# Bringing the last tiles' outputs to their tokens: scatter and reload, or products with one-hot matrices

## The chip, the cores and the metric

The kernel runs on one core of a Trainium2 chip. A core has a matrix engine (TensorE, "PE"; its weight loads are "PEld"), a vector engine (VectorE, "DVE"), an engine for activation functions (ScalarE, "ACT"), a general engine (GpSimd, "POOL") and a queue engine (SyncE, "SP"), each with its own program, kept together by semaphores. Sixteen DMA engines move data between HBM, where inputs and outputs lie, and SBUF, the on-chip memory of 128 partitions. PE writes to PSUM, a second on-chip memory of eight banks; DVE and ACT read it.

The metric is the time of one execution on the device in microseconds (us). A profiled execution lists every instruction with its start and duration, in us from the span's start.

## The reference, cut to what matters

There are 8 batches of 256 tokens with 128 channels, all float32. Two blocks follow one another. The first adds attention-pooled tokens that went through eight experts with a threshold on the gates; in the second each token is adapted, normalised (`xn`; the adapted token is also the `residual`) and sent to its two best of eight experts:

```python
x = x + _L0_ffn_ref(_L0_cond_ref(x, ...), ...)
x = x + _L1_ffn_ref(_L1_cond_ref(x, itok_B_0_8, ...), ...)
...
    probs = jax.nn.softmax(jnp.einsum('bld,de->ble', xn, gate_w), axis=-1)
    w, idx = jax.lax.top_k(probs, TOP_K)
    w = w / jnp.sum(w, axis=-1, keepdims=True)
    cw = jnp.sum(w[..., None] * jax.nn.one_hot(idx, E, dtype=x.dtype), axis=2)
    h = jax.nn.gelu(jnp.einsum('bld,edh->eblh', xn, w1) + b1[:, None, None, :], approximate=False)
    out_e = jnp.einsum('eblh,ehd->ebld', h, w2) + b2[:, None, None, :]
    output = jnp.einsum('ble,ebld->bld', cw, out_e)
    return output + residual
```

So each of the 2048 output tokens is a residual plus two expert outputs, each multiplied by its weight.

## The kernel before, in words

The first block runs densely: 16 tiles of 128 tokens in five units (`UNITS`), every expert for every token, with two stages of products a unit (`layer`, lines 872 to 907). As units end, `adapt` (line 649) normalises their tokens, picks the two experts of each, and GpSimd scatters each token twice into a buffer `xs` in HBM, sorted by expert. With each copy go the row of the output buffer `ys` where its result belongs (`xt[:, D]`) and its weight (`xt[:, D + 1]`). Row number 2 * token + s of `ys` holds the s-th of a token's two results, so the even number next to it names the token.

The second block is sparse. Tiles of 128 sorted rows of one expert are listed as they fill: `SLOTS` is the number of tiles known after units 2, 3 and 4 (17, 21, 39). At most 39 tiles can be needed; the program runs the first 36 (`SURE`) always, and the last three inside a branch (`tc.If`, line 1074) on the count of tiles. A tile goes through four functions:

- `fetch` (line 920): SP loads the tile's rows from `xs` (64 KB and a little) and the expert's first weights (256 KB).
- `turn` (line 955): PE transposes, DVE scales into `xc` and copies the bias `b1`.
- `hidden` (line 964): DVE makes `b2`, PE four products `hps`, ACT four Gelu `hs`.
- `output` (line 977): PE four products `yps`, DVE adds bias and weight into `yt` (line 985), and GpSimd scatters the 128 rows of `yt` into `ys` (line 986).

A product of 128x128 by 128 columns in float32 stands in the trace as two PE instructions. In the main loop a tile is fetched five tiles ahead (`LEAD`) and its stages run two tiles apart (`AHEAD`); a planner orders the engines' work by its own costs there. When the loop over 36 tiles ends, `hidden` of tiles 34 and 35 and `output` of 32 to 35 are left.

The full tiles of the early batches come first in the lists. From tile 31 on (`SETTLED`) none of the outputs belongs to the first six batches (`EARLY`). So, once tile 30's scatter has landed, SP loads these six batches' rows of `ys` (`load`, line 1002, 256 KB a batch), and DVE adds both results to the residual (`add`, line 1009, two additions of 128x256). After the scatter of tile 35 come: three stores on SP, the branch over the spare tiles, the loads of the last two batches in halves on SP and ACT, the other three stores, the additions of the four halves, and their stores.

From line 1057 on an order written out by hand (`tc.manual_schedule`) holds for DVE, ACT and POOL; PE and SP stay with the planner. Every engine's queue runs in order: an SP instruction that waits holds back all stores and loads behind it.

Of the kernel before, what the change touches and what calls it, by code (L numbers as in the profile page):

```python
# [22 lines left out]
B, S, D = 8, 256, 128  # L23
P = 128
NT = B * S // P
NG = 4
GT = NT // NG
GN = GT * P
# [16 lines left out]
NSLOT = SLOTS[NU - 1]  # L45
SURE = 36
EARLY = 6


SETTLED = max(SLOTS[NU - 2] + E, 4 * EARLY + E - 1)  # L50
NOWHERE = 1 << 20
SEARCH = 16
SEARCH_GAP = 3
# [30 lines left out]
def tile_adaln_ffn_d2(ctx: ExitStack, tc: tile.TileContext, x, ptype, lang, cols, b1v,  # L84
                      w10, w20, w11d, w21d, lw1, lw2, lgb, out):
    nc = tc.nc
# [25 lines left out]
    ident = const.tile([P, P], F32, name="ident")  # L112
# [478 lines left out]
    for e in range(E):  # L591
        nc.sync.dma_start(out=w21[:, e, :], in_=w21d[e].rearrange("p c d -> p (c d)"))
    nc.sync.dma_start(out=b2all.rearrange("p e d -> p (e d)"),
                      in_=b2d.rearrange("e d -> (e d)").partition_broadcast(P))
    rows = xs.rearrange("(p m t) c -> p m (t c)", p=P, t=GT)
    nc.sync.dma_start(out=rows, in_=empty.rearrange("p t c -> p (t c)").unsqueeze(1).to_broadcast(list(rows.shape)))

# [357 lines left out]
    def turn(k, xt, wt):  # L955
        tp = pss.tile([P, P], F32, tag="sm", name=f"xtp{k}")
        nc.tensor.transpose(tp, xt[:, :D], ident)  # L957
        xc = work.tile([P, P], F32, tag="xc", name=f"xc{k}", bufs=AHEAD + 3)
        nc.vector.tensor_scalar(xc, tp, col[:, C_LG:C_LG + 1], col[:, C_LB:C_LB + 1], ALU.mult, ALU.add)  # L959
        b1 = small.tile([P, HC], F32, tag="b1", name=f"b1_{k}", bufs=AHEAD + 3)  # L960
        nc.vector.tensor_copy(b1, b1all[:, bass.ds(number(k), 1), :].rearrange("p o c -> p (o c)"))  # L961
        return k, xt, wt, xc, b1

    def hidden(k, xt, wt, xc, b1):
        hp = psb.tile([P, HC, P], F32, tag="big", name=f"hps{k}")
        hT = work.tile([P, HC, P], F32, tag="scr", name=f"hs{k}", bufs=NSCR)

        b2 = work.tile([P, GN], F32, tag="gbc", name=f"b2_{k}", bufs=4)[:, :D]
        nc.vector.tensor_tensor(b2, b2all[:, bass.ds(number(k), 1), :].rearrange("p o d -> p (o d)"),
                                xt[:, D + 1:D + 2].to_broadcast([P, D]), ALU.mult)  # L970
        for c in range(HC):
            nc.tensor.matmul(hp[:, c, :], lhsT=wt[:, c * P:(c + 1) * P], rhs=xc, start=True, stop=True)  # L972
        for c in range(HC):
            nc.scalar.activation(hT[:, c, :], hp[:, c, :], AF.Gelu, bias=b1[:, c:c + 1])  # L974
        return k, xt, hT, b2

    def output(k, xt, hT, b2):
        ek = expert(k, PE)
        yp = psy.tile([P, D], F32, tag="y", name=f"yps{k}")
        for c in range(HC):  # L980
            nc.tensor.matmul(yp, lhsT=hT[:, c, :], rhs=w21[:, bass.ds(ek, 1), c * D:(c + 1) * D],  # L981
                             start=(c == 0), stop=(c == HC - 1))

        yt = first.tile([P, HC, D], F32, tag="w2", name=f"yt{k}")[:, 0, :]
        nc.vector.scalar_tensor_tensor(yt, yp, xt[:, D + 1:D + 2], b2, ALU.mult, ALU.add)  # L985
        move = nc.gpsimd.indirect_dma_start(  # L986
            out=ys, out_offset=bass.IndirectOffsetOnAxis(ap=xt.bitcast(I32)[:, D:D + 1], axis=0),
            in_=yt, in_offset=None, bounds_check=2 * NT * P - 1, oob_is_err=False)
        tc.declare_no_dep(move.ins, group="outputs", reason="no two outputs share a row")
        tc.add_to_no_dep_group("outputs", move.ins)  # L990
        if k >= SETTLED:
            tc.declare_no_dep(move.ins, group="settled", reason="no more outputs for the first batches")
        if k == SETTLED - 1:
            for n in range(EARLY):
                load(n, slice(0, 2), nc.sync, "settled")
# [6 lines left out]
    def load(n, part, queue, group=None):  # L1002
        y = work.tile([P, 2, 2 * D], F32, tag="scr", name=f"yg{n}_{part.start}", bufs=NSCR)[:, part, :]
        move = queue.dma_start(out=y, in_=yv[n, :, part, :])
        if group:
            tc.add_to_no_dep_group(group, move.ins)
        loaded.append((n, part, y))

    def add():
        n, part, y = loaded.popleft()  # L1010
        o = resid[n // 2][:, n % 2 * 2 + part.start:n % 2 * 2 + part.stop, :]

        tc.keep_in_program_order(nc.vector.tensor_tensor(o, y[:, :, :D], o, ALU.add))
        tc.keep_in_program_order(nc.vector.tensor_tensor(o, o, y[:, :, D:], ALU.add))
        return n, part, o

    def store(queue, n, part, o):
        tc.keep_in_program_order(queue.dma_start(out=of[n][:, part, :], in_=o))

    fetched, flipped, hid = deque(), deque(), deque()  # L1020

    def proceed(ahead, between=lambda: None):
        if len(flipped) > ahead:
            hid.append(hidden(*flipped.popleft()))
        between()
        if len(hid) > ahead:
            output(*hid.popleft())
# [20 lines left out]
    for k in range(PRIMED, SURE):  # L1048
        ahead(k + LEAD)
        if k == SLOTS[NU - 2]:  # L1050

            while len(flipped) > 1 or len(hid) > 1:
                proceed(1)
        flipped.append(turn(*fetched.popleft()))
        pump()
        proceed(AHEAD, pump)

    ending = ExitStack()
    ending.enter_context(tc.manual_schedule(engines={DVE, ACT, POOL}))
    while flipped or hid:  # L1060
        if flipped:
            hid.append(hidden(*flipped.popleft()))
        while len(hid) > bool(flipped) + 1:
            output(*hid.popleft())
        if not flipped:
            output(*hid.popleft())
    while behind:
        pump()
    sums = [add() for _ in range(EARLY)]
    for _ in range(3):  # L1070
        store(nc.sync, *sums.pop(0))
    more = nc.values_load(tiles[0][0:1, 0:1], engines=(SP, PE, DVE, ACT, POOL), min_val=0, max_val=NSLOT,
                          skip_runtime_bounds_check_because="a count of tiles")
    with tc.If(more > SURE - SLOTS[NU - 2]):
        for k in range(SURE, NSLOT):
            output(*hidden(*turn(*fetch(k))))
    ending.close()
    queues = itertools.cycle((nc.sync, nc.scalar))
    for n in range(EARLY, B):
        for t in range(2):  # L1080
            load(n, slice(t, t + 1), next(queues))
    queues = itertools.cycle((nc.scalar, nc.sync))
    for done_sum in sums:
        store(next(queues), *done_sum)
    while loaded:
        store(next(queues), *add())


# [48 lines left out]
```

## Time and profile before

| what | value |
| --- | --- |
| median of 6 runs | 361.79 us (360.47 to 363.86) |
| profiled execution, its own time | 364.55 us |
| span of its instructions | 362.5 us |
| mean granted PE clock | 0.975 |
| busy PE / DVE / ACT / POOL | 337.5 / 202.7 / 155.9 / 97.0 us |
| moved by DMA | 47.19 MB, 130 GB/s on average |

The profile page divides the span into 40 slices and shows each engine's busy share of a slice in tenths, with the granted PE clock in tenths of full speed. A timeline lists instructions as start, duration, engine, source line, operation, output and inputs, how many were merged, and the idle time of the engine before with what ended it. The chain of waits goes back from the last instruction to what released each step. A window's row has the stretch, its length, the busy time of PE, PEld, DVE, ACT and POOL (with the number of instructions), the granted clock, the share of time the DMA engines were busy, and GB/s. Starts and ends of PE instructions are modelled: its records overlap, and their spacing tells more than their length.

### The profile page before, as it was taken

The numbers are of one execution on the slowest core, as the hardware profiler recorded it, in microseconds if no ns is written. First come the engines' busy times: TensorE is split into PE (matmuls) and PEld (weight loads), VectorE is DVE, ScalarE is ACT, GpSimd is POOL, SyncE is SP. The second block draws the span as 40 slices with busy tenths as digits, with TensorE's granted clock in tenths as the row PEclk, the third lists the DMA queues.
The fourth block names the chain that finished last, engine by engine and source line by source line (L and its number), as shares of the span: only waits on it lengthen the run. The fifth ranks groups of instructions, "written<-read, shape, count | busy, mean of one in ns | idle before, by whom it ended". The sixth has DMA issues, their size and how long they took to land.

```text
span 362.5 us, 5961 instructions
## 1 busy us (share of the span) xinstructions
PE 337.5 (93%) x1628; PEld 222.6 (61%) x1628; DVE 202.7 (56%) x868; ACT 155.9 (43%) x354; POOL 97.0 (27%) x150
## 2 busy tenths in 40 slices
PE   8999999999999999999999999998999877999930
PEld 7885444444444444444445688876879777999920
DVE  3674755623046666575512474786787656544453
ACT  4375455445434343324433355435544514564610
POOL 7500000000000120650170021073136563545540
PEclk9999999999999999999999999999999996999985
DMA  6882799907023210221120111124653654676174
GB/s 191 278 284 74 216 375 380 322 7 201 31 87 104 63 38 29 66 53 56 32 66 22 29 31 44 31 74 114 192 158 94 175 154 109 199 198 199 56 238 136
DMA packets 35417, 47.19 MB, mean 130 GB/s; under 512 B 5562, under 2 KB 18446, under 8 KB 35384
## 3 DMA queue, kind: packets, MB, share of 16 engines
q1 hardware_dynamic: 31640, 41.26, 37.9%
q0 software_dynamic: 2304, 4.37, 3.5%
q10 hardware_dynamic: 1440, 1.18, 1.0%
q8 instruction: 14, 0.23, 0.3%
q14 instruction: 19, 0.16, 0.2%
HBM read 32.66 MB, written 14.39 MB: 130 GB/s over the span
## 4 chain that ended last, share of the span: by engine, by line
PE 79%; DVE 8%; POOL 3%; issue 3%; DMA 2%; another core or an unknown queue 2%; ACT 1%; DVEq 0%; POOLq 0%; SPq 0%
PE hp_first L897 28%; PE yp_first L877 26%; PE yps L981 7%; PE hps L972 7%; PE poolp L358 2%; POOL xs L784 2%; PE idle L219 1%; ACT hs L974 1%; DMA ys<-yt,xt 1%; PE g0p L254 1%; DMA yg<-ys 1%; PE xtp L957 1%; PE xTp L231 1%; DVE sofar L756 1%
## 5 line engine op out<-in xcount | busy, mean ns | idle before, releaser
L899 ACT ACTIVATE hT_first<-hp_first,col 128x512 f32<-128x512 f32 (+1 forms) x160 | 92.6, 602 | 93.8 <-PE hp_first L897 90.0
L897 PE MATMUL hp_first<-poolT,w 128*128 128x512 f32 (+1 forms) x320 | 119.9, 512 | 0.8 <-ACT hT_first L899 0.8
L877 PE MATMUL yp_first<-hT_first,w 128*128 128x512 f32 (+1 forms) x320 | 119.7, 512 | 0.0
L897 PEld LDWEIGHTS hp_first<-poolT,w 128*128 128x128 f32 x320 | 58.6, 190 | 45.7 <-issue 40.4
L877 PEld LDWEIGHTS yp_first<-hT_first,w 128*128 128x128 f32 x320 | 58.7, 190 | 45.3 <-issue 41.0
L974 ACT ACTIVATE hs<-hps,b 128x128 f32<-128x128 f32 x144 | 40.0, 376 | 40.9 <-PE hps L972 10.9
L784 POOL DMA_INDIRECT xs<-zr,pos x32 | 31.6, 986 | 66.0 <-DVE pos L782 30.9
L986 POOL DMA_INDIRECT ys<-yt,xt x36 | 36.6, 1018 | 38.0 <-DVE yt L985 26.3
L981 PE MATMUL yps<-w,hs 128*128 x288 | 39.6, 284 | 2.7 <-DVE ek L627 1.5
L972 PE MATMUL hps<-xc,wt 128*128 128x128 f32 x288 | 39.8, 281 | 2.4 <-issue 2.4
L865 DVE SCALAR_TENSOR_TENSOR part_first<-yp_first,col,gbc_first 128x512 f32<-128x512 f32 (+1 forms) x28 | 17.2, 614 | 40.7 <-PE yp_first L877 39.4
L981 PEld LDWEIGHTS yps<-w,hs 128*128 128x128 f32 x288 | 36.5, 199 | 3.3 <-ACT hs L974 3.0
L972 PEld LDWEIGHTS hps<-xc,wt 128*128 128x128 f32 x288 | 36.0, 196 | 3.2 <-issue 3.1
L550 POOL TENSOR_TENSOR rstd_l<-ve_l,nhalf 128x4 f32<-128x4 f32 (+1 forms) x5 | 5.0, 1008 | 69.0 <-DVE ve_l L548 68.0
L867 DVE TENSOR_TENSOR acc_first<-acc_first,part_first 128x512 f32<-128x512 f32 (+1 forms) x35 | 20.1, 580 | 0.5
L961 DVE COPY b<-col 128x4 f32 x36 | 6.5, 185 | 23.2 <-ACT hs L974 20.1
L985 DVE SCALAR_TENSOR_TENSOR yt<-yps,xt,b 128x128 f32<-128x128 f32 x36 | 12.4, 348 | 10.9 <-PE yps L981 10.3
L484 POOL DMA_DIRECT2D gd_L<-gT_L x1 | 0.7, 668 | 63.9 <-DVE gT_L L482 63.9
L885 ACT ACTIVATE y_first<-yp_first,col 128x512 f32<-128x512 f32 x8 | 5.5, 687 | 23.2 <-PE yp_first L877 14.6
L959 DVE TENSOR_SCALAR xc<-xtp,col 128x128 f32<-128x128 f32 x36 | 14.4, 402 | 0.8 <-PE xtp L957 0.4
L499 DVE TENSOR_SCALAR_CACHE_REDUCE fl<-logit,tr 128x128 bf16<-128x128 f32 x46 | 13.5, 343 | 0.6
L518 DVE TENSOR_SCALAR_CACHE_REDUCE ok<-kt 128x3 f32<-128x3 f32 (+1 forms) x16 | 2.6, 160 | 13.8 <-PE kt L502 13.8
(224 smaller groups left out, 296.7 us busy)
## 6 DMA issues: line engine op xcount, KB each, us to landing
wt<-in_w_dram SPq DMA_DIRECT2D x36, 256.0 KB
xs<-empty SPq DMA_DIRECT2D x1, 8580.0 KB
w<-in_w_dram SPq DMA_DIRECT2D x24, 256.0 KB
gbc_first<-gd_L SPq DMA_DIRECT2D x24, 256.0 KB
xt<-xs SPq DMA_DIRECT2D x36, 65.0 KB
gbc_first<-gd_L SPq DMA_DIRECT2D x16, 128.0 KB
yg<-ys SPq DMA_DIRECT2D x6, 256.0 KB
xg<-in_x_dram SPq DMA_DIRECT2D x8, 128.0 KB
```

Source lines behind the costliest of these rows:

```text
L499: nc.vector.tensor_scalar(flags, lflat, values[:, i:i + 1], None, ALU.is_lt, ALU.add, accum_out=c[:, i:i + 1])
L784: move = nc.gpsimd.indirect_dma_start(out=xs, out_offset=bass.IndirectOffsetOnAxis(ap=pos[:, t:t + 1], axis=0), in_=zr[s][:, t, :], in_off ...
L865: nc.vector.scalar_tensor_tensor(part, y, bias, gbc, ALU.add, ALU.mult)
L867: nc.vector.tensor_tensor(accs[u], accs[u], part, ALU.add)
L877: nc.tensor.matmul(yp, lhsT=w2s[e][:, c, :], rhs=hT[:, c, :], start=(c == 0), stop=(c == HC - 1))
L897: nc.tensor.matmul(hp, lhsT=w1s[e][:, c * P:(c + 1) * P], rhs=sources[g][:, o * P:o * P + n], start=True, stop=True)
L899: nc.scalar.activation(hT[:, c, :], hp, act, bias=col[:, cb1 + e * HC + c:cb1 + e * HC + c + 1])
L959: nc.vector.tensor_scalar(xc, tp, col[:, C_LG:C_LG + 1], col[:, C_LB:C_LB + 1], ALU.mult, ALU.add)
L972: nc.tensor.matmul(hp[:, c, :], lhsT=wt[:, c * P:(c + 1) * P], rhs=xc, start=True, stop=True)
L974: nc.scalar.activation(hT[:, c, :], hp[:, c, :], AF.Gelu, bias=b1[:, c:c + 1])
L981: nc.tensor.matmul(yp, lhsT=hT[:, c, :], rhs=w21[:, bass.ds(ek, 1), c * D:(c + 1) * D], start=(c == 0), stop=(c == HC - 1))
L986: move = nc.gpsimd.indirect_dma_start(out=ys, out_offset=bass.IndirectOffsetOnAxis(ap=xt.bitcast(I32)[:, D:D + 1], axis=0), in_=yt, in_off ...
```

## The change

The last three tiles that always run (33 to 35, from `PLACED = SURE - 3` on) no longer scatter. Instead:

- `turn` of such a tile calls `home`: DVE makes, from the row numbers, a one-hot matrix of 128 rows by the 512 tokens of the last two batches (the even row number is compared with a table `places`, written once by an iota on POOL before tile 30's `turn`).
- `brought` multiplies, on PE, the transposed one-hot slices with `yt`: four products a tile, which add up in two PSUM banks (`late`), one a batch.
- The rows of `ys` of the last two batches are filled with zeros at the start, since not all of them will be written; SP loads them, whole batches at a time, after tile 32's scatter.
- `gathered` joins on PE: identity times residual, identity times the first results, identity times the second, 128x256 each, into PSUM. Of the six early batches the first four are still added on DVE, the other two (`ADDED = 4`) are joined in this way in banks of their own; of the last two, the joins go on in the banks of `brought`. ACT copies three of the four results out of PSUM, DVE the last.
- The tile count is read inside the main loop, the branch over the spare tiles comes last, after all these stores; inside it the spare tiles' outputs go through `brought` too, are added and stored again.
- The hand-written order now holds for PE and SP as well.

In the diff, the conditions on `k >= PLACED` stand in `turn`, after `xc`, and in `output`, after `yt`.

```diff
+PLACED = SURE - 3
+LATE = B - EARLY
+ADDED = 4
...
+    for n in range(EARLY, B):
+        nc.sync.dma_start(out=ys[n * 4 * P:(n + 1) * 4 * P, :].rearrange("(p t) d -> p t d", t=GT), in_=empty[:, :, :D])
...
+        if k >= PLACED:
+            home(k, xt)
...
+        if k >= PLACED:
+            return k, yt
...
+    def gathered(sums, begin):
+        n, part, y, o = taken_up()
+        for i, some in enumerate((o, y[:, :, :D], y[:, :, D:])):
+            nc.tensor.matmul(sums, lhsT=ident, rhs=some, start=begin and not i, stop=i == 2)
+        return n, o
...
+    def home(k, xt):
+        even = small.tile([P, 1], I32, tag="even", name=f"even{k}", bufs=2)
+        nc.vector.tensor_scalar(even, xt.bitcast(I32)[:, D:D + 1], -2, None, ALU.bitwise_and)
+        at = small.tile([P, 1], F32, tag="atf", name=f"atf{k}", bufs=2)
+        nc.vector.tensor_copy(at, even)
+        homes[k] = work.tile([P, GN], F32, tag="acc", name=f"home{k}", bufs=3)
+        nc.vector.tensor_scalar(homes[k], places[0], at, None, ALU.is_equal)
+    def brought(k, yt, sums, begin, end=False):
+        for i in range(GT):
+            nc.tensor.matmul(sums[i // 2][:, i % 2, :], lhsT=homes[k][:, i * P:(i + 1) * P], rhs=yt,
+                             start=begin and i % 2 == 0, stop=end and i % 2 == 1)
...
-    while flipped or hid:
...
-    sums = [add() for _ in range(EARLY)]
-    for _ in range(3):
-        store(nc.sync, *sums.pop(0))
+    hid.append(hidden(*flipped.popleft()))
+    output(*hid.popleft())
+    placed = [output(*hid.popleft())]
+    hid.append(hidden(*flipped.popleft()))
+    store(nc.sync, *add())
+    for n in range(EARLY, B):
+        load(n, slice(0, 2), nc.sync)
+    placed.append(output(*hid.popleft()))
+    late = pairs("late")
+    brought(*placed[0], late, True)
+    store(nc.sync, *add())
+    placed.append(output(*hid.popleft()))
+    brought(*placed[1], late, False)
+    brought(*placed[2], late, False)
+    for _ in range(ADDED - 2):
+        store(nc.sync, *add())
+    for _ in range(ADDED, EARLY):
+        held = psy.tile([P, 2, D], F32, tag="y", name=f"held{loaded[0][0]}")
+        n, o = gathered(held, True)
+        nc.scalar.copy(o, held)
+        store(nc.sync, n, o)
+    lasts = [gathered(some, False) for some in late]
+    for (n, o), some, copy, queue in zip(lasts, late, (nc.scalar.copy, nc.vector.tensor_copy), (nc.scalar, nc.sync)):
+        copy(o, some)
+        store(queue, n, o)
     with tc.If(more > SURE - SLOTS[NU - 2]):
+        rest = pairs("rest")
         for k in range(SURE, NSLOT):
-            output(*hidden(*turn(*fetch(k))))
+            brought(*output(*hidden(*turn(*fetch(k)))), rest, k == SURE, k == NSLOT - 1)
+        for (n, o), some in zip(lasts, rest):
+            nc.vector.tensor_tensor(o, some, o, ALU.add)
+            store(nc.sync, n, o)
     ending.close()
-    queues = itertools.cycle((nc.sync, nc.scalar))
-    for n in range(EARLY, B):
-        for t in range(2):
-            load(n, slice(t, t + 1), next(queues))
-    queues = itertools.cycle((nc.scalar, nc.sync))
-    for done_sum in sums:
-        store(next(queues), *done_sum)
-    while loaded:
-        store(next(queues), *add())
```

More of the change, by code (lines that the diff above doesn't have):

```diff
@@ L50 @@
 SETTLED = max(SLOTS[NU - 2] + E, 4 * EARLY + E - 1)
+PLACED = SURE - 3
+LATE = B - EARLY
+ADDED = 4
+assert PLACED >= SETTLED and LATE * 2 == GT
 NOWHERE = 1 << 20
@@ L1009, in add, with taken_up, store, pairs @@
     def add():
-        n, part, y = loaded.popleft()
[L1011 to L1018, printed above, removed]
+        n, part, y, o = taken_up()
+        nc.vector.tensor_tensor(o, y[:, :, :D], o, ALU.add)
+        nc.vector.tensor_tensor(o, o, y[:, :, D:], ALU.add)
+        return n, o
+    def taken_up():
+        n, part, y = loaded.popleft()
+        return n, part, y, resid[n // 2][:, n % 2 * 2:n % 2 * 2 + 2, :]
+    def gathered(sums, begin):
+        n, part, y, o = taken_up()
+        for i, some in enumerate((o, y[:, :, :D], y[:, :, D:])):
+            nc.tensor.matmul(sums, lhsT=ident, rhs=some, start=begin and not i, stop=i == 2)
+        return n, o
+    def store(queue, n, o):
+        queue.dma_start(out=of[n], in_=o)
+    homes = {}
+    def home(k, xt):
[9 more added lines that the diff above has]
+                             start=begin and i % 2 == 0, stop=end and i % 2 == 1)
+    def pairs(name):
+        return [psb.tile([P, 2, D], F32, tag="big", name=f"{name}{i}") for i in range(LATE)]
+    places = []
     fetched, flipped, hid = deque(), deque(), deque()
@@ L1053, in tile_adaln_ffn_d2 @@
                 proceed(1)
+        if k == SETTLED - 1:
+            places.append(work.tile([P, GN], F32, tag="part", name="places"))
+            tc.keep_in_program_order(nc.gpsimd.iota(
+                places[0], pattern=[[4 * P, LATE], [2, 2], [4, P]], base=EARLY * 4 * P, channel_multiplier=0,
+                allow_small_or_imprecise_dtypes=True))
+            more = nc.values_load(tiles[0][0:1, 0:1], engines=(SP, PE, DVE, ACT, POOL), min_val=0, max_val=NSLOT,
+                                  skip_runtime_bounds_check_because="a count of tiles")
         flipped.append(turn(*fetched.popleft()))
@@ L1056, in tile_adaln_ffn_d2 @@
         proceed(AHEAD, pump)
-    ending = ExitStack()
-    ending.enter_context(tc.manual_schedule(engines={DVE, ACT, POOL}))
-    while flipped or hid:
[L1061 to L1066, printed above, removed]
     while behind:
         pump()
-    sums = [add() for _ in range(EARLY)]
-    for _ in range(3):
-        store(nc.sync, *sums.pop(0))
@@ L1072, in tile_adaln_ffn_d2 @@
-    more = nc.values_load(tiles[0][0:1, 0:1], engines=(SP, PE, DVE, ACT, POOL), min_val=0, max_val=NSLOT,
-                          skip_runtime_bounds_check_because="a count of tiles")
+    ending = ExitStack()
+    ending.enter_context(tc.manual_schedule(engines={PE, DVE, ACT, POOL, SP}))
+    hid.append(hidden(*flipped.popleft()))
[5 more added lines that the diff above has]
+        load(n, slice(0, 2), nc.sync)
```

## The prediction

> **What bounds the kernel now.** I read the busy slices first, then the chain of waits over the last 18 us, then the timelines of DVE, POOL and SP there, and last the windows of that stretch. The slices say that TensorE (PE) is full until the 38th of 40 and then stops, so everything up to about 344 us is PE's and the rest is a tail:
>
> ```profile
> PE   8999999999999999999999999998999877999930
> PEclk9999999999999999999999999999999996999985
> ```
>
> The tail's chain, from the last matmuls on:
>
> ```profile
> 344.54 2.20 PE yps L981 x16
> ...
> 346.99 0.35 DVE yt L985
> ...
> 349.90 4.31 DMA ys<-yt,xt
> ...
> 354.80 3.60 DMA yg<-ys
> ...
> 359.28 0.29 DVE resid L1014
> ```
>
> The reader sees two DMA flights, 4.3 and 3.6 us, one after the other: tile 35's scatter lands at 354.21, only then are the last two batches' rows loaded, and 359.57 + 2.9 of store and closing make the span of 362.5. From the last matmul (ends 348.35) to the end it is 14.2 us without PE. The timeline shows who else uses the DMA engines then:
>
> ```profile
> 342.17 1.08 POOL L986 DMA_INDIRECT ys<-yt,xt  x1 [1.47 <-DVE yt L985]
> 344.53 2.74 SPq L1004 DMA_DIRECT2D yg<-ys  x6
> 344.90 0.97 POOL L986 DMA_INDIRECT ys<-yt,xt  x1 [0.37 <-issue]
> 351.38 0.42 DVE L1013 TENSOR_TENSOR resid<-yg,resid 128x256 f32<-128x256 f32 x1 [1.03 <-issue]
> 356.95 0.29 DVE L1013 TENSOR_TENSOR resid<-yg,resid 128x128 f32<-128x128 f32 x1 [2.31 <-DMA yg<-ys]
> ```
>
> Tile 30's scatter starts at 342.17 and lets the six early loads go at 344.53. Tile 32's starts at 344.90, under these loads. DVE idles 1.03 us before the third early batch: it came at 351.4. The windows give the DMA engines' load (last two columns):
>
> ```profile
> 348.50:352.00 3.50, 0.00 (x0) 0.00 (x0) 2.37 (x7) 0.00 (x0) 1.95 (x2) 0.93 0.87 308
> 352.00:354.30 2.30, 0.00 (x0) 0.00 (x0) 2.20 (x7) 0.00 (x0) 0.00 (x0) 0.50 0.23 77
> ```
>
> They are nearly full until 352, with the six early loads.
>
> **The change part by part.** All times are of the profiled execution: span 362.5, its own time 364.55, that is 0.8% over the median of 361.79. I work out a difference in it and take that from the median.
>
> *Main loop.* Two zero fills (256 KB each) go ahead of the fill of xs on SP. At the 360 GB/s of 55 to 72 us they cost 1.5 us, at a third of it 4.4; the queue is empty (5 GB/s) from 72 to 74 and the next work on it, the gate rows, starts at 80.8. Hidden, and 4.4 us still fit. The iota (128x512) on POOL is put between scatters: nearest rows 0.64 us (affine_select of 128x512) and 0.18 (iota of 39 columns); POOL spends 1.27 of each 1.89 us a tile, so 0.64 is made up within two tiles. The load of the tile count moves to tile 30: 0.27 to 0.51 us an engine (its rows at L1072), hidden on ACT, POOL, SP and DVE, and PE reads one such number per tile already. It leaves SP's wait of the tail, where it cost 1.3 us with its branch but ran out just as the scatter landed. `home` gives DVE three more instructions in each of tiles 33 to 35: 0.15 (128x1, L520), 0.16 (128x1, L522) and 0.69 (128x512, L863), 1.0 us a tile. DVE sat idle 2.43 us before 341.55 and 1.60 before 344.27 waiting for PE, so two fit there; the third delays yt of tile 32, by 0 to 1.0 us. I take 0.3. Without that cover it would be 1.0 more on scatter 32.
>
> *Scatters 33 to 35 go.* Three POOL instructions of 0.97 + 0.30 and the 4.31 us flight leave the chain. What the late loads wait for is now tile 32's scatter. Its landing is bounded by the fastest row, 342.17 to 344.5 (2.4 us, DMA engines idle), and the slowest, 349.90 to 354.21 (4.3 us, under loads). It flies under the six loads, so I take 4.3: 344.90 + 0.3 + 4.3 = 349.5, from 347.3 to 350.2. SP also stands behind the first add (0.85 us after early load 1 lands; 349.5 at the latest, by DVE's own row). So the late loads issue at 349.6 and 350.0 instead of 354.35: 4.7 us earlier.
>
> *But they queue.* Six early batches of 256 KB are ahead on the same queue. Third landed at 351.4; at 308 GB/s a batch is 0.85 us, so by rate the fifth lands at 353.1, the sixth at 353.9, late ones at 354.8 and 355.6. The 77 GB/s after 352 says most of the bytes were through by then, which puts the fifth as early as 352. Lower end for the late ones: 349.6 + the 4.05 us that 354.35 to 358.40 shows, 353.65. I take 352.6 for the fifth and 354.5 for the late ones. That they go out on SP alone and not on SP and ACT: two issues of 0.36 after one another instead of beside, inside the wait for data.
>
> The Trainium skill, page "DMA: Bandwidth & Descriptors", section "Issuing engines are not separate DMA queues", says the same of the queues: DMAs of whichever engine share the 16 DMA engines, so the change of queue should neither win nor lose bandwidth. Our row does not separate the two queues; by the page this edit is 0.
>
> *PE's new work.* After tile 34's output, PE puts four products (128x128 fp32) for each placed tile: as many as hps, x8 in 0.89 us, so 2.7 us for three. They wait for yt33 (346.72 to 347.05 in the trace, where PE had run dry at 346.3), yt34 behind add 0 on DVE (348.3), and yt35 behind add 1 (349.5 + 0.85 + 0.35 = 350.7), so the third ends at 351.6. Before the fifth load (352.6), PE thus waits: all this is hidden. Then two early and two late batches, three products of 128x256 each, six instructions. By the 128x512 and 128x256 rows of the first layer (88.8 us for 192; 31.1 for 128) and the spacing of 0.111 for 128 columns, a 256-column instruction is 0.22 to 0.24 us: 1.38 us a batch. The residual product of batch 5 runs ahead, so from 352.6: 0.92 + 3 x 1.38 = 357.7. The late loads (354.5 + 0.92 + 1.38 = 356.8) are not the limit; PE's order is. This replaces two DVE adds of 0.3 us a half batch, which ended 0.9 us after the last load: the join on PE is the dearer one, and PE begins the late batches only after the early two.
>
> *Behind it.* PE to DVE under 0.1 us when PE has run dry (yps ends at 348.35, yt starts at 348.39), copy of 128x256 from PSUM 0.42 (DVE rows of that shape): 358.2, against 359.57. ACT's copies of batches 5 to 7 (0.41 each, its 128x256 copy) run beside. Then 2.95 us to the end as now, plus two things: the last store is 128 KB instead of 64 KB (64 KB more at the last slice's 136 GB/s are 0.5 us, with the queue empty nearer 0; I take 0.3), and the branch over the spare tiles now comes after the stores. On SP the branch and its seven semaphore steps spread over 353.03 to 354.04, 1.0 us; part runs beside the store's flight, part may come behind its landing: 0 to 1.0, taken 0.4.
>
> Sum: 358.2 + 2.95 + 0.3 + 0.4 = 361.85 against 362.5: 0.65 us won, of 4.7 us by which the loads start earlier. 361.79 - 0.65 = 361.1.
>
> A rule against the change: the skill's page "TensorE: Matmul & The Clock Gate", section "Part 1: The HAM clock gate", says that PE's clock is halved after an idle window of about 3.4 us. The trace agrees: PE is busy 1.2 of the 4 us from 298 to 302, and the granted clock is 0.65 in 300 to 301 and 0.50 after it; in the old tail it is 0.93 in 348.5 to 352 and then 0.50. By the rule a wait of 1 us before the joins costs nothing, and one beyond 3.4 us doubles them.
>
> **The rivals.**
>
> *Loads do not hold the joins (faster).* Without three scatters and two stores among them the early loads may land back to back, the fifth before 351. Then PE goes through from the third placed tile: yt35 at 350.0, its products until 350.9, 4 x 1.38 = 356.4, copy at 357.1, end at 357.1 + 2.95 + 0.3 = 360.4 with the branch beside the store; with add 1 a further 1 us earlier, 359.4. That is 2.1 to 3.1 won: 358.7 to 359.7. For it: 77 GB/s after 352, a thin remainder. Against it: the idle 1.03 us on DVE at 351.4, at a time when the DMA engines show 0.87 busy.
>
> *PE goes cold (slower).* If PE idles long before the joins, the eight-instruction group that takes 1.06 us takes 2.05, as at 301.88 (clock 0.50). The 5.06 us of joins after 352.6 would become 9.7: +4.7, 365.8 by the median. It decides once PE has waited some 3 us, that is with the fifth load at 354.6 or later. Against it: between 346 and 351.6 PE has 3.6 us of work, more than the 1.2 of 4 that went with the drop.
>
> *Signals of PE come late (slower).* In the trace ACT starts hs of tile 35 at 346.55, 2.0 us after its products ended (344.5), and DVE waits 1.9 and 2.4 us in the same way; each time PE was streaming on. If the joins run in one stream the held batches' copies all fall behind it: three ACT copies (1.2 us) and three stores on SP in order (0.36 each) instead of one. Then the last store leaves about 1.1 us later and the gain of 0.65 turns into 0.45 lost: 362.2, and with the longest such wait of DVE, 2.4 us, on top: 364.6.
>
> *Nothing is moved.* The late loads are behind the early ones anyway, and join and branch eat the rest: 361.8, inside the main case.
>
> **How the numbers follow.** Main case (with the last rival in it) 0.46; its own range is 359.6 to 362.6, from the fifth load at 352.0 or 353.1 (-0.6, +0.5), 0.22 or 0.24 us an instruction (-0.2, +0.2), and the ends of store (-0.3, +0.2) and branch (-0.4, +0.6). Loads not holding the joins 0.31. Cold PE 0.08, late signals 0.15. Half a per cent, about what a measurement of this kernel can tell, is 1.8 us: 359.98 and 363.6. Faster: the second case, 0.31. Slower: cold PE and two thirds of late signals, 0.18. Same: the main case and the rest of late signals, 0.51. The range runs from the far end of the second case to the middle of late signals' span and leaves out cold PE: 358.6 to 364.0.
>
> **What would show it.** Right: late loads issued near 350; no scatter after tile 32; PE waiting for yg near 352, its last join ending near 357.5 at a clock of 1.00; the last PSUM copy on DVE near 358. Wrong: yg in SBUF before PE finishes the placed tiles (faster), a granted clock of 0.50 in 352 to 358, ACT's copies bunched behind the last join, a scatter 32 that lands after 351, or tile 31's products on PE later than 340.8, which would mean that the main loop was disturbed.

## The result, and the profile after

The changed kernel takes 364.6 us (median of 24 runs, 361.64 to 369.13), against 361.65 for the kernel before (50 runs on the same chip, 359.90 to 363.86). The ratio is 1.0079, with a 95% interval of 1.0063 to 1.0096: 2.95 us slower, where 0.65 us faster was forecast, and 0.6 us beyond the upper end of the range. By the prediction's own bound of half a per cent this is "slower". That had a chance of 0.18, but on the strength of two reasons in the tail, not of the one that came true. The ratio leaves out the run of 369.13 us, which lies 2% above the fastest.

The two profiled executions alone would have said the opposite: the changed kernel's span is 360.6 us and its own time 362.35, the other's were 362.5 and 364.55. The difference lies in a stretch that the change does not touch. In the windows view (stretch, length, busy PE, PEld, DVE, ACT, POOL with counts, granted clock, DMA share, GB/s) the kernel before shows

```profile
290.00:310.00 20.00, 15.71 (x111) 15.06 (x111) 11.63 (x61) 6.62 (x24) 9.94 (x11) 0.83 0.51 140
```

and the changed one

```profile
290.00:310.00 20.00, 15.98 (x123) 15.33 (x123) 11.71 (x60) 7.17 (x27) 10.73 (x11) 0.91 0.46 134
```

PE stands idle in parts of this stretch, and the clock drops, in one execution further than in the other. Counted by `yt`, which each tile makes once, the kernel before is 0.3 us behind at the tenth tile (293.34 against 293.00) and 2.6 behind at the 25th (330.09 against 327.54). From there to the end the changed kernel takes 33.1 us and the other 32.4, so this pair shows only 0.65 us of the loss. So whole profiles say little here; stretches do.

The changed kernel's busy slices, to be compared with those in the prediction:

```profile
PE   7999999999999999999999999998999976999895
...
PEclk9999999999999999999999999999999998999999
```

The old tail of nearly empty PE slices is gone, as foreseen. New is the 8 in slice 38 of 40 (333.6 to 342.6 us): inside the main loop, where the kernel before had nines from slice 35 to 38. By windows, before:

```profile
330.00:340.00 10.00, 9.90 (x89) 9.74 (x88) 5.67 (x23) 5.35 (x20) 5.35 (x6) 1.00 0.50 153
```

and after:

```profile
330.00:340.00 10.00, 8.18 (x70) 7.67 (x69) 5.72 (x25) 4.38 (x16) 4.62 (x5) 1.00 0.45 129
```

PE stands still for 1.82 us there, at full clock. Who holds it up is read from the changed kernel's timelines (start, duration, engine, line, operation, tiles; in brackets the idle time before and what ended it). First DVE:

```profile
328.13 0.28 DVE L979 TENSOR_TENSOR b<-b2all,xt 128x128 f32<-128x128 f32 x1
331.18 0.15 DVE L1045 TENSOR_SCALAR even<-xt 128x1 int32<-128x1 int32 x1 [2.77 <-DMA xt<-xs]
...
331.60 0.35 DVE L995 SCALAR_TENSOR_TENSOR yt<-yps,xt,b 128x128 f32<-128x128 f32 x1
332.68 0.15 DVE L1045 TENSOR_SCALAR even<-xt 128x1 int32<-128x1 int32 x1 [0.73 <-DMA xt<-xs]
...
333.85 0.88 DVE L1049 TENSOR_SCALAR home<-places,atf 128x512 f32<-128x512 f32 x2 [0.37 <-POOL places L1097]
```

`even`, the first instruction of `home` for tile 33, stands in DVE's queue ahead of `yt` of tile 25. It needs nothing but tile 33's rows, and the planner put it as early as its own costs allowed. DVE reaches it at 328.41; SP issues that load only at 328.73:

```profile
328.73 0.33 SPq L936 DMA_DIRECT2D xt<-xs  x1
```

and it lands 2.4 us later. Until then DVE does nothing, though the product that `yt` of tile 25 needs was finished at 328.80. `even` of tile 34 does the same once more for 0.73 us, and `home` then waits 0.37 us for the table `places`, whose iota stands on POOL behind the scatter of that same `yt`:

```profile
332.22 0.97 POOL L998 DMA_INDIRECT ys<-yt,xt  x1 [2.97 <-DMA xt<-xs]
333.20 0.62 POOL L1097 IOTA places<- 128x512 f32 x1
```

PE works off what it has in hand and then stops three times: 0.40, 0.25 and 1.17 us, together the 1.82.

```profile
332.09 1.13 PE L991 MATMUL yps<-w,hs 128*128 x8 [0.40 <-ACT hs L984]
333.47 0.33 PE L965 MATMUL xtp<-ident,xt 128*128 128x128 f32 x1 [0.25 <-DVE atf L1047]
...
335.86 1.13 PE L991 MATMUL yps<-w,hs 128*128 x8 [1.17 <-DVE yt L995]
```

The Trainium skill says of this, on the page "PSUM — Partial Sum Buffer", section "Engine vs sequencer instructions", that the queues of ScalarE, VectorE and GpSimdE are strict FIFO. The rows agree: for 2.77 us DVE ran nothing that stood behind `even`.

The tail, in the chain of waits, did change as the diff says:

```profile
349.14 1.84 PE late L1054 x16
350.98 2.66 PE held L1034 x12
353.64 2.70 PE late L1034 x12
356.34 0.02 issue
356.36 0.42 DVE resid L1133
```

Both DMA flights are off the chain; PE goes from the placed products into the joins. The late loads are issued at 350.20. PE's weight loads wait 0.20 us for the fifth early load and 0.23 for the late ones; the products behind them come no more than 0.1 us later for it:

```profile
350.20 0.80 SPq L1016 DMA_DIRECT2D yg<-ys  x2
...
351.21 0.73 PEld L1034 LDWEIGHTS held<-yg,ident 128*128 128x128 f32 x4 [0.20 <-DMA yg<-ys]
...
353.89 0.73 PEld L1034 LDWEIGHTS late<-yg,ident 128*128 128x128 f32 x4 [0.23 <-DMA yg<-ys]
```

From the end of DVE's copy at 356.78 it is 3.8 us to the end of the span; before it was 2.9 from the end of the last addition.

### The profile page after: what moved, and what is told of

It is laid out like the page before. It is cut to its first block, busy times and chain, and to the rows that moved or that the text cites. A ratio compares the mean times of both kernels' runs of the same rounds, so it can differ in the third digit from the quotient of the medians.

```text
span 360.6 us, 6037 instructions
## 1 busy us (share of the span) xinstructions
PE 343.9 (95%) x1676; PEld 227.6 (63%) x1676; DVE 201.5 (56%) x866; ACT 157.3 (44%) x357; POOL 94.7 (26%) x148
## 4 chain that ended last, share of the span: by engine, by line
PE 79%; DVE 8%; POOL 4%; issue 3%; another core or an unknown queue 2%; DMA 2%; ACT 1%; DVEq 1%; SPq 0%; POOLq 0%
PE hp_first L905 28%; PE yp_first L885 26%; PE yps L991 7%; PE hps L982 6%; PE poolp L364 2%; POOL xs L792 2%; PE g0p L260 1%; DMA col<-in_cols_dram 1%; PE xtp L965 1%; ACT hs L984 1%; DVE sofar L764 1%; PE late L1054 1%; PE late L1034 1%; PE held L1034 1%
## 5 line engine op out<-in xcount | busy, mean ns | idle before, releaser
L998 POOL DMA_INDIRECT ys<-yt,xt x33 | 33.7, 1020 | 36.5 <-DVE yt L995 23.7
L982 PE MATMUL hps<-xc,wt 128*128 128x128 f32 x288 | 39.0, 278 | 2.0 <-issue 2.0
L965 PE MATMUL xtp<-ident,xt 128*128 128x128 f32 x36 | 9.7, 280 | 0.8 <-issue 0.6
```

Source lines behind the costliest of these rows:

```text
L998: move = nc.gpsimd.indirect_dma_start(out=ys, out_offset=bass.IndirectOffsetOnAxis(ap=xt.bitcast(I32)[:, D:D + 1], axis=0), in_=yt, in_off ...
```

## The experiments

Theory A: the blocked DVE queue in the loop is the whole loss, and the tail by itself is a gain. Theory B: the tail is slower than it looks. Theory C: the two zero fills disturb the first block. The kernels of one group ran on one chip, together with the kernel before, and every ratio is against that kernel's runs on the same chip. The groups differ: the kernel before took 361.65 us beside the result, 354.77 in the first group below, and 359.55, 354.81 and 354.47 in the later ones.

### The order of `home`, the loop alone, the fills alone

`pin` is the changed kernel with the three instructions of `home` held where the program has them, after `xc` of their own tile:

```diff
+        pinned = tc.keep_in_program_order if k < SURE else lambda ins: ins
...
-        nc.vector.tensor_scalar(even, xt.bitcast(I32)[:, D:D + 1], -2, None, ALU.bitwise_and)
+        pinned(
+            nc.vector.tensor_scalar(even, xt.bitcast(I32)[:, D:D + 1], -2, None, ALU.bitwise_and))
...
-        nc.vector.tensor_copy(at, even)
+        pinned(nc.vector.tensor_copy(at, even))
...
-        nc.vector.tensor_scalar(homes[k], places[0], at, None, ALU.is_equal)
+        pinned(nc.vector.tensor_scalar(homes[k], places[0], at, None, ALU.is_equal))
```

> The changed kernel, with the three instructions of home held behind the scale of their own tile in DVE's queue (the planner had put them three tiles earlier). Theory A, a blocked DVE queue: the loss lies in the loop, and the new tail is 2.7 us shorter by the profiles (from the first product of tile 34 to the end 18.1 against 20.8 us); so this kernel is faster than before, about 359.0 us against 361.65, and DVE no longer waits for xt ahead of xc of tile 30. Theory B, the new tail or the late branch is slow outside a profile: it stays near 364. Theory C, the zero fills: it stays near 364 as well.

`loop_only` is the kernel before with the iota and `home` in the loop and nothing that uses them:

```diff
+        if PLACED <= k < SURE:
+            home(k, xt)
...
+        if k == SETTLED - 1:
+            places.append(work.tile([P, GN], F32, tag="part", name="places"))
+            tc.keep_in_program_order(nc.gpsimd.iota(
```

> The kernel before, with home (iota and three DVE instructions in each of tiles 33 to 35) added to the loop and not used; tail and fills as before. Theory A: it carries the whole loss of the loop without the gain of the tail, 2.9 + 2.7 = 5.6 us slower than before, some 367 us, and at least 2.9 slower; in its trace DVE waits for xt and PE idles after 330 us. Theories B and C: as before, 361.7, at most 0.5 more.

`fill_only` is the kernel before with the two fills:

```diff
+    for n in range(EARLY, B):
+        nc.sync.dma_start(out=ys[n * 4 * P:(n + 1) * 4 * P, :].rearrange("(p t) d -> p t d", t=GT), in_=empty[:, :, :D])
```

> The kernel before, with the two zero fills of ys added and nothing else. Theories A and B: no difference, 361.7 +- 0.5, because the queue is empty for 8 us after the fills. Theory C: near 364.5, with the gate rows or PE late after 70 us.

| kernel | median, us | ratio to before (95%) |
| --- | --- | --- |
| before | 354.77 | |
| pin | 352.45 | 0.9947 (0.9918 to 0.9977) |
| loop_only | 357.04 | 1.0067 (1.0039 to 1.0095) |
| fill_only | 354.00 | 0.9977 (0.9950 to 1.0004) |

The fills cost nothing that can be measured, so C falls. The loop's part alone costs 2.4 us (1.4 to 3.4), less than half of the 5.6 expected and under the 2.9 that was named as the least, and shows the same waits as the changed kernel, here in the view of waits (engine, line, waited for: total us, times, longest):

```profile
POOL ys L990 <- DMA xt<-xs: 3.9, 1, 3.9
DVE even L1029 <- DMA xt<-xs: 3.7, 1, 3.7
...
PE yps L985 <- DVE yt L989: 2.6, 2, 1.5
...
DVE home L1033 <- POOL places L1072: 1.1, 1, 1.1
```

With `home` held in its place PE has no gap in the loop. The windows of `pin`:

```profile
320.00:330.00 10.00, 10.00 (x92) 10.00 (x92) 5.46 (x23) 6.22 (x23) 6.43 (x7) 1.00 0.77 218
330.00:340.00 10.00, 10.00 (x92) 10.00 (x91) 6.30 (x23) 4.74 (x17) 4.01 (x4) 1.00 0.43 139
```

against `loop_only`:

```profile
320.00:330.00 10.00, 7.57 (x66) 7.22 (x65) 3.83 (x18) 5.51 (x20) 3.66 (x4) 1.00 0.76 209
```

and the whole change then gains 1.9 us (0.8 to 2.9 by the interval of the ratio). That is A: the same instructions, three tiles later in the queue, turn a loss into a gain. B falls. The stall can be read in every profile as the time from `yt` of tile 24 to `yt` of tile 30: 11.01 to 11.02 us in `pin`, its two repeats below and `fill_only`, 11.46 in the kernel before, but 13.71 in the changed kernel and 14.09 in `loop_only`. Held in place, `home` thus costs nothing that shows in this stretch. The gain of the tail does not show in `pin`'s own profile, whose time is 1.6 us over the kernel's median and where PE waits 1.10 us for the fifth early load: from `yt` of tile 24 to the end it takes 31.38 us, `fill_only` 31.32. The two repeats take 30.27 and 30.02.

### How large the loss is, on one chip

For this the changed kernel ran again, beside `pin`.

> The changed kernel itself, beside the pinned one on one chip. Theory (the blocked DVE queue is the whole loss): slower than before by 0.5 to 1.1%, and above the pinned kernel by what the loop alone lost on another chip, 2.4 us, up to 4.8 us, which is what the ratios 1.0079 and 0.9947, measured on two chips, would give. Rival (part of the loss sits in the tail, by chip): within 1 us of the pinned kernel.

> The pinned kernel again, as the one that the others of this job are compared with: 0.992 to 0.998 of before. If the tail's gain depended on the first chip, it would lie within 0.2% of before here.

The changed kernel: 363.21 us, ratio 1.0094 (1.0065 to 1.0123); the pinned one: 358.58, ratio 0.9975 (0.9953 to 0.9996); before 359.55. So the order of three small instructions a tile is worth 4.6 us by the medians, 4.3 by the ratios. In the changed kernel's profile of this chip `even` reaches the head of DVE's queue 0.5 us before its load is issued, and `home` waits longer for `places`:

```profile
330.55 0.15 DVE L1045 TENSOR_SCALAR even<-xt 128x1 int32<-128x1 int32 x1 [3.73 <-DMA xt<-xs]
...
333.29 0.88 DVE L1049 TENSOR_SCALAR home<-places,atf 128x512 f32<-128x512 f32 x2 [1.12 <-POOL places L1097]
```

```profile
327.30 0.33 SPq L936 DMA_DIRECT2D xt<-xs  x1
```

PE is busy for 7.09 of the 10 us from 330 to 340 there, 10.00 in the pinned kernel. These 2.9 us are not all of the 4.6. From `yt` of tile 24 to `yt` of tile 30 the loop loses 3.65 us (14.67 against 11.02). Part of the rest is seen in the tail, where PE waits for the fifth early load in the changed kernel

```profile
351.54 1.13 PE L1034 MATMUL held<-yg,ident 128*128 128x256 f32 x4 [0.84 <-DMA yg<-ys]
```

and not in the pinned one, whose joins follow the placed products without a gap:

```profile
346.33 0.60 PE L1034 MATMUL held<-resid,ident 128*128 128x256 f32 x2
346.77 1.03 PE L1034 MATMUL held<-yg,ident 128*128 128x256 f32 x4
347.63 0.59 PE L1034 MATMUL held<-resid,ident 128*128 128x256 f32 x2
```

Another part is in the closing, from the last store's issue to the end: 4.45 us against 3.68, of which more below. From `yt` of tile 24 to the end the two profiles differ by 5.26 us. That the stall causes the two parts in the tail is not shown: `pin`, without a stall, has a wait of 1.10 us at the same place, and `iota_first` below, with a stall, has none.

The early loads leave 3.5 us after `yt` of tile 30 in the changed kernel (344.10 against 340.63), 2.9 in the pinned one (339.52 against 336.60). In the changed kernel's two profiles `yt` of tiles 29 and 30 come 0.8 us apart, so the scatter of tile 30 stands behind that of tile 29 on POOL. In `loop_only` and `iota_first` they come 1.9 us apart in spite of the stall, and the loads leave after 3.0. The loop alone lost 2.4 us on its chip; by the profiles of `loop_only` and `fill_only` it is 3.1 us up to `yt` of tile 30 and 2.7 to the end.

### Which of the two waits

`iota_first` is the changed kernel with the iota issued at the sixth tile ahead of where it was; DVE's order of `even` stays.

```diff
-        if k == SETTLED - 1:
+        if k == SETTLED - 6:
             places.append(work.tile([P, GN], F32, tag="part", name="places"))
...
+        if k == SETTLED - 1:
             more = nc.values_load(tiles[0][0:1, 0:1], engines=(SP, PE, DVE, ACT, POOL), min_val=0, max_val=NSLOT,
```

> The changed kernel with the iota that writes places issued six tiles earlier, so that home never waits for it; even stays where the planner put it, ahead of tiles 30 to 32 in DVE's queue. It parts the two waits that DVE showed in the changed kernel: 3.73 us of even for tile 33's rows and 1.12 us of home for places. Theory (the row load at the head of the queue is the cause): 0 to 1.1 us faster than the changed kernel, so still 2 to 4 us above before and 3.2 us or more above the pinned kernel. Rival (the iota behind the scatters is the cause): within 1 us of the pinned kernel.

> The pinned kernel, as the one that the others of this job are compared with: 0.993 to 0.999 of before.

It took 356.21 us, ratio 1.0038 (1.0007 to 1.0070); the pinned kernel beside it 352.80, ratio 0.9952 (0.9923 to 0.9981); before 354.81. `home` waits for nothing now, `even` as long as ever:

```profile
326.31 0.15 DVE L1045 TENSOR_SCALAR even<-xt 128x1 int32<-128x1 int32 x1 [3.52 <-DMA xt<-xs]
326.50 0.15 DVE L1047 CAST atf<-even 128x1 f32<-128x1 int32 x1
326.76 0.49 DVE L1049 TENSOR_SCALAR home<-places,atf 128x512 f32<-128x512 f32 x1
```

So the wait for the rows alone costs 3.4 us by the medians, 3.1 by the ratios, and 2.7 from `yt` of tile 24 to the end of the two profiles (32.71 against 30.02). The 3.2 us or more above the pinned kernel that were expected hold by the medians; above the kernel before it is 1.4 us, where 2 to 4 were expected. The wait for the table is the remainder, about 1.2 us, from a difference between two chips and so only an estimate.

### What sets the end of the joins

The prediction had PE's order as the limit: the two late batches are joined behind the two early ones. `pin_added6` adds all six early batches on DVE (`ADDED = 6`), so PE has two joins instead of four.

> Pinned, and all six early batches are added on DVE, so PE joins only the two late ones. The prediction's step 'PE's order is the limit' (the late batches' joins start only after the two early ones, 1.35 us each): PE is free for the late joins as soon as they land, 1.0 to 2.7 us faster than the pinned kernel, less what the two more adds on DVE (1.2 us) take. Rival (the late loads are the limit, PE waits for them anyway): within 0.5 us of the pinned kernel. If DVE's two more adds stand ahead of its copy of the last batch, up to 1.2 us slower.

359.66 us, ratio 0.9994 (0.9968 to 1.0020), beside 358.58 for the pinned kernel (0.9975): not faster; it is 1.1 us slower by the medians and 0.7 by the ratios, whose intervals overlap. PE is free early and waits for the loads instead:

```profile
347.38 0.60 PE L1034 MATMUL late<-resid,ident 128*128 128x256 f32 x2
349.90 1.13 PE L1034 MATMUL late<-yg,ident 128*128 128x256 f32 x4 [1.93 <-DMA yg<-ys]
```

From `yt` of tile 35 to the end of the last join it is 6.84 us here (345.79 to 352.63) and 6.93 in `pin_again` (344.75 to 351.68). PE's four joins and the loads end almost together, so taking work from PE alone gains nothing. The closing is also longer in this profile: 4.17 us from the last store's issue, against 3.43, 3.68 and 3.44 in the three profiles of the pinned kernel.

### The closing

`pin_nobranch` leaves the branch over the spare tiles out.

> Pinned, without the branch over the three spare tiles, whose body these inputs never enter (the spare tiles are left out). It prices the branch that now comes after the stores: the prediction's term is 0.4 us, between 0 and 1.0. Over 1.0 us faster: the late branch cost more than its bounds. Within 0.2 us: it is hidden beside the last store.

357.68 us, ratio 0.9932 (0.9909 to 0.9955), beside 358.58 (0.9975): the late branch costs 0.9 us by the medians and 1.5 by the ratios. The reason is in SP's list of instructions (start, duration, operation, line). With the branch:

```
352.168 0.332 DMA_DIRECT2D L1038 out_dram<-resid
352.540 0.276 TENSOR_LOAD L1102 <-total
352.875 0.050 COMPARE_BRANCH L1137
...
354.132 0.017 EVENT_SEMAPHORE L1137
354.200 0.028 EVENT_SEMAPHORE L1191
...
354.883 0.028 EVENT_SEMAPHORE L1191
```

and without it:

```
353.998 0.332 DMA_DIRECT2D L1038 out_dram<-resid
354.376 0.017 EVENT_SEMAPHORE L1184
...
354.984 0.028 EVENT_SEMAPHORE L1184
355.716 0.028 EVENT_SEMAPHORE L1184
```

Where there is no branch, eleven of twelve closing steps of 0.06 us run beside the store's 1.7 us flight, and only the twelfth waits for it. Where there is one, SP goes through the branch's steps until 354.13, and the twelve come after it. From the last store's issue to the end of the span (355.85 and 356.66): 3.68 us with the branch, 2.67 without. In the kernel before it was 2.89 with half the store, and the step that waits for that store ended 1.56 us after its issue, 1.72 here. So the larger store costs 0.2 us at most.

Two attempts to win this back. `pin_act` gives the last store to ACT, so that SP can pass the branch early, and `pin_act5` adds a fifth early batch on DVE (`ADDED = 5`).

```diff
-    for (n, o), some, copy, queue in zip(lasts, late, (nc.scalar.copy, nc.vector.tensor_copy), (nc.scalar, nc.sync)):
+    for (n, o), some, copy, queue in zip(lasts, late, (nc.scalar.copy, nc.vector.tensor_copy), (nc.scalar, nc.scalar)):
```

> Pinned, with the very last store (DVE's copy of the eighth batch) issued by ACT instead of SP. In the pinned kernel's trace SP, after this store's issue, goes alone through the branch and its semaphores (352.50 to 354.13) and the closing ones (to 354.95), while the same store's landing was waited for until 355.72 where there was no branch, 1.7 us after its issue. Theory (SP's queue after the last issue is the closing's limit): SP does the branch while PE still joins, the closing falls from 3.7 us to about 2.7, 0.6 to 1.2 us faster than the pinned kernel. Rival (every engine's branch, or the store's flight, sets the end): within 0.3 us.

> As the one before, with five early batches added on DVE and one joined on PE. PE's joins of 1.3 us each are then three instead of four. If PE's order sets the end: 1.3 us faster than with four added. If the late loads do (with all six added PE waited 1.93 us for them): 0 to 0.5 us faster.

353.80 us (ratio 0.9965, 0.9935 to 0.9995) and 353.92 (0.9965, 0.9935 to 0.9996), beside 352.80 for the pinned kernel: no gain from either. In `pin_act` SP now stands still at its last step of the branch until 351.55, 1.78 us after ACT's issue of the store at 349.77, and then goes through its twelve steps:

```
349.773 0.350 DMA_DIRECT2D L1038 out_dram<-resid
...
351.552 0.017 EVENT_SEMAPHORE L1137
...
352.303 0.028 EVENT_SEMAPHORE L1191
```

In the trace the semaphore of that step at 351.55 is the one that tells of this store's landing, and so it is in the pinned kernel at 354.13: the end of the branch waits for the store itself. The closing stays at 3.50 us, and the theory that SP's own pace was the limit falls. In `pin_act5` PE waits in each of its three joins, and they end 6.5 us after `yt` of tile 35 (341.19 to 347.73) instead of 6.9: again the loads, 0.4 us ahead of what four joins need. These 0.4 us are lost behind the joins: the last store's step ends 2.48 us after its issue, and the closing takes 4.20. From issue to that step it was 1.71 to 1.96 in the three profiles of the pinned kernel, 2.45 in `pin_added6` and 2.73 in the changed kernel beside `pin_again`. Why the landing is late there stays open.

`pin_mid` puts the branch between the placed products and the joins.

```diff
     brought(*placed[2], late, False)
+    with tc.If(more > SURE - SLOTS[NU - 2]):
+        for k in range(SURE, NSLOT):
+            brought(*output(*hidden(*turn(*fetch(k)))), late, False)
```

> Pinned, with the branch over the spare tiles moved from behind the last stores to between the third placed tile's products and PE's joins (its body then adds into the same PSUM banks). The branch then lies on PE's stream, SP's wait at its end comes before the stores, and the closing should shrink to the 2.7 us after the last store's issue that the kernel without a branch showed, against 3.4 to 3.7. Theory (the closing's wait for the last store at the branch's end costs 0.8 to 1.0 us, and PE's own branch is short, 0.5 us or less): 0.3 to 1.0 us faster than the pinned kernel, so 0.990 to 0.996 of before. Rival (every engine stops at the branch, the joins start later by its whole 1 to 1.6 us): 0 to 1 us slower than pinned, 0.996 to 1.001 of before.

354.09 us against 354.47 for the kernel before, ratio 0.9982 (0.9954 to 1.0010). The closing shrinks to 2.69 us (347.68 to 350.37), but PE goes through the branch and starts its joins late,

```profile
341.77 0.67 PE L1034 MATMUL held<-resid,ident 128*128 128x256 f32 x2 [0.45 <-DVE resid L1024]
```

and they end 7.6 us after `yt` of tile 35 (339.57 to 347.19) instead of 6.9. The rival's range holds: what the closing wins, PE's order gives back.

The pinned kernel is as fast as any here that computes all: 0.9947, 0.9975 and 0.9952 of before on three chips (0.9 to 1.9 us), and 4.6 us faster than the changed kernel where both ran.

## Why the prediction was wrong

**The step that failed** is the main loop: "`home` gives DVE three more instructions in each of tiles 33 to 35 ... so two fit there; the third delays yt of tile 32 ... I take 0.3", bounded by 1.0 us. I priced the instructions by their duration and laid them into DVE's idle time of the old trace, as if they stood where the program has them. The durations were right or high (0.15, 0.15 and 0.48 us against 0.15, 0.16 and 0.69). What they wait for and what is queued behind them was not asked: in this loop the planner decides their place, and it puts them three tiles early, in front of a load that SP has not yet issued. Measured, 4.6 us between the two orders on one chip; in the order that I had assumed they cost nothing that shows up to tile 30 (11.02 us from `yt` of tile 24 against 11.01 in `fill_only`). The iota failed in the same way: its 0.62 us were priced well (0.64), but it stands behind a scatter, and `home` on DVE waits for it. No rival had either: cold PE and late signals, the two slower cases, both lie in the tail. The list of signs at the prediction's end named a disturbed main loop as a way to be wrong, but gave it no chance and no price. The range has a slip of its own: the middle of the late signals' span, 362.2 to 364.6, is 363.4, not 364.0.

**The fills** were costed at nothing, rightly.

**The late loads.** Forecast for 349.6, measured 350.20, 4.15 us earlier than before against 4.7. SP stood from 348.78 on at a wait for tile 32's scatter, issued at 345.82. The step holds.

**The joins.** Forecast 1.38 us a batch from 256-column rows of the first layer; in a stream they follow one another at 1.30 (`pin_again`: 346.33, 347.63, 348.93). The wait for the fifth load was put at 1.0 us before the joins; it was 0.20 (of the weight loads alone) and 0.84 in the changed kernel's two profiles, and 1.10, none and none in the pinned kernel's three. So the rival "loads do not hold the joins" had the wait right in three of these five, but not the gain: 0.9 to 1.9 us instead of 2.1 to 3.1. "PE's order is the limit" holds by a hair only: with one or two joins fewer the joins end 0.1 to 0.4 us earlier, because the loads stand just behind.

**The closing.** The larger store was put at 0.3 us and is 0.2 at most; the branch at 0.4 and is 0.9 to 1.5 by the times, 1.0 by the two closings. Its upper bound of 1.0 was about the measured value. I had part of it run beside the store's flight; so it does, but its end waits for the store, and twelve steps that are hidden without a branch follow.

**The cold clock** did not come. The granted clock is 1.00 through the joins' beginning, and PE hardly waits:

```profile
352.00:354.30 2.30, 2.30 (x12) 1.86 (x11) 0.00 (x0) 0.74 (x2) 0.00 (x0) 1.00 1.00 336
```

**Late signals of PE** did not come: ACT's copies start at 352.38, 353.67 and 355.12, as far apart as the joins, and do not bunch behind the last.

**The sum.** For the tail alone 0.65 us won was forecast. With the loop's stall taken away the change wins 0.9 to 1.9 us, so the tail was underrated by 0.3 to 1.3, the shorter waits and joins more than paying for the dearer branch. The loop's 4.6 us turned that into a loss.

## What to carry to other kernels

An added instruction is priced by three things: its duration, what it waits for, and what stands behind it in its engine's queue. Where a planner orders the queue, an instruction that depends only on a load far ahead is apt to be put far ahead of its use; ask of each one when its load is issued, and hold it in program order if that is later than the work around it. And before work is taken from one limit, look how near the next one is: here PE's joins and the loads ended within 0.4 us of one another, and two edits that relieved PE gained nothing.

## What the runs showed of the hardware that was not expected

- One DVE instruction of 0.15 us that waits for a 65 KB load stops DVE for 2.8 to 3.7 us. Alone, in `iota_first`, it costs 3.1 to 3.4 us of the kernel's time (2.7 by the two profiles): more than the 0.9 to 1.9 us that the whole change of the tail wins.
- A branch whose body is not entered costs about 1 us behind the last store, since its end waits for that store's landing (the wait ends 1.7 to 2.7 us after the issue) and the closing steps come after. In front of PE's joins PE's idle time was 0.45 us and the joins ended 0.7 us later.
- The same kernel took 361.65 us beside the result, and 359.55 and 354.47 in two of the groups. The record names the same chip for these two groups, so it is not shown that the chip makes the difference. Most of it lies in one stretch: from the tenth `yt` to the eleventh it is 8.0 us in the kernel before and 8.2 in the changed kernel beside the result, 6.5 to 7.0 in the group with 359.55, and 2.9 to 3.1 in the groups near 354.5. In `fill_only`, one of the last, PE shows no wait from 290 to 310 and has its full clock:

```profile
290.00:310.00 20.00, 20.00 (x181) 20.00 (x181) 14.45 (x68) 12.34 (x44) 13.96 (x15) 1.00 0.67 183
```

Why the wait is absent there stays open.
